# Where the keys' sums of squares are formed in a two-layer attention kernel: four single-column matmuls, or a transposing sum and the fold matmul

## The chip, the cores and the metric

The kernel runs on one core of one Trainium2 chip. The metric is the device time of one execution in microseconds (us), median of several runs. The core has a matrix engine (TensorE, "PE" in the profile, with its weight loads shown apart as "PEld"), and four others that work beside it, each through its own queue in order: VectorE (DVE), ScalarE (ACT), GpSimd (POOL) and SyncE (SP), which issues most of the transfers. Matmul results go to PSUM, everything else lies in SBUF.

## The reference

32 sequences of 64 tokens with 512 features go through two layers; each is a cross attention and a feed-forward part with residual sums. All is in 32-bit floats. What matters here is the second layer's attention, which normalises every query and every key by its root mean square before the scores:

```python
def rmsnorm(x, w, eps=EPS):
    xf = x.astype(jnp.float32)
    var = jnp.mean(xf * xf, axis=-1, keepdims=True)
    return w * (xf * jax.lax.rsqrt(var + eps)).astype(x.dtype)
...
q = rmsnorm(q, q_norm_w)
k = jnp.repeat(k, n_rep, axis=1)
v = jnp.repeat(v, n_rep, axis=1)
k = rmsnorm(k, k_norm_w)
scale = 1.0 / np.sqrt(HEAD_DIM)
scores = jnp.einsum('bhqd,bhkd->bhqk', q, k) * scale + attention_mask
attn = jax.nn.softmax(scores.astype(jnp.float32), axis=-1).astype(q.dtype)
out = jnp.einsum('bhqk,bhkd->bhqd', attn, v)
```

There are 32 query heads and 8 key heads of 128 features. The sum of squares is over these 128 features, so there is one sum for each query of each head and one for each key.

## The kernel before

The 2048 tokens are cut into four chunks of 512 (eight sequences). Each attention layer walks through 32 steps: for each of the 8 key heads `g` the four chunks `c`. A step makes the keys (`project_k`), the four query heads of the group (`project_q`), the values' sum (`values`), the value projection (`project_v`), the first products of the output projection (`output_first`) and the scores of the next step (`scores`); the rest of the output products (`output_rest`) and the softmax, cut into pieces by `yield`, run between them. `run` is software-pipelined: in the turn of step i the keys and queries of step i+1 are projected before the values of step i are formed. A scheduler places the instructions in each engine's queue by the order of the code and waits are by semaphores; each queue is then worked in order.

The names that matter:

- **kT, ksq.** `project_k` (L333) leaves the keys transposed in PSUM: 128 features on the partitions, 512 keys along the row. In the second layer ACT squares them into `ksq` (L355) and DVE scales them into `kT` (L356).
- **quarters, part.** The query projection (L188, tiles `P`) is a seven-product scheme whose result comes in four quarters, called in the order in which the matmuls end. For each, DVE adds two pieces into `qT` (L416), ACT squares that (L418), and DVE makes `part` (L422): a reduction with `apply_transpose=True`, which transposes each 32x32 block and sums along the row, so that 128x512 squares give 128x16 sums over 32 features each. Four such calls fill `part`.
- **pm, fold.** `norms` (L430) puts sums over all 128 features into the PSUM tile `pm`, 20 columns: 16 for the queries, 4 for the keys. For the keys, four matmuls (L440) take a 128x128 block of `ksq` as weights and the column of ones as moving operand. For the queries, four matmuls (L446), j = 0 to 3, take `fold` as weights (128x32, four stacked 32x32 identities), 16 columns of `part` as moving operand, and write 32 rows of `pm` each, so that each uses another group of 32 columns of the array. A 32-bit matmul appears in the trace as two passes, each with a weight load and a matmul: the 4 calls of either kind are 8 loads and 8 matmuls.
- **qs, qr, rb.** DVE copies `pm` with a small constant to `qs` (L456), POOL raises it to the power -1/2 into `qr` (L231), and DVE spreads the queries' part over the columns as `rb` (L280). The keys' part of `qr` and `rb` are multiplied into the scores (L502).

On PE's queue a step of the second layer runs: pk (L340), P (L188), po (`values`, L564), pm (L440, then L446), pv (L366), the first two output products O (L188), S (`scores`, L468), the other five products O. After `qr` POOL forms four sums of blocks of `oT` (`left_sums`, L168 to L171), which output products use; after them it adds the mask to the scores (L512).

Of the kernel before, what the change touches and what calls it, by code (L numbers as in the profile page):

```python
# [9 lines left out]
F32 = mybir.dt.float32  # L10
# [5 lines left out]
ALU = mybir.AluOpType  # L16
AX = mybir.AxisListType

P = 128
# [8 lines left out]
NH = NB // 4  # L28
KB = 32
KH = S // KB  # L30
# [14 lines left out]
def tile_xattn_ffn_2_layers(ctx: ExitStack, tc: tile.TileContext, a: dict, out: bass.AP):  # L45
    nc = tc.nc
# [5 lines left out]
    const = ctx.enter_context(tc.tile_pool(name="const", bufs=1))  # L52
# [3 lines left out]
    sm = ctx.enter_context(tc.tile_pool(name="sm", bufs=2))  # L56
    psp = ctx.enter_context(tc.tile_pool(name="psp", bufs=6, space=bass.MemoryType.PSUM))

    def mm_tile(name):
        return psp.tile([P, CH], F32, tag="mm", name=name)  # L60
# [25 lines left out]
    def tmp_tile(name):  # L86
        return ap_.tile([P, 2, CH], F32, tag="tmp", name=name)
# [15 lines left out]
    def load_ctx(c, name):  # L103
        t = ctx_tile(f"ctxT{name}")
        nc.sync.dma_start(
            t, a["ctxT"][:, c * CH : (c + 1) * CH].rearrange("(k p) t -> p k t", p=P)
        )
        return t
# [37 lines left out]
    fold = const.tile([P, KB], F32, tag="fold", name="fold")  # L146
    nc.gpsimd.memset(fold, 0.0)
    for j in range(4):
        nc.vector.tensor_copy(fold[j * KB : (j + 1) * KB, :], ident[j * KB : (j + 1) * KB, j * KB : (j + 1) * KB])
    ones = const.tile([P, 1], F32, tag="ones", name="ones")  # L150
    nc.gpsimd.memset(ones, 1.0)
    wqk = const.tile([P, 2], F32, tag="wqk", name="wqk")

    def key_weight():
# [10 lines left out]
    def left_sums(t, width=HC, engine=nc.gpsimd):  # L165
        b = [t[:, k, :, 0:width] for k in range(NBLK)]
        tt = engine.tensor_tensor
        tt(b[4], b[2], b[3], ALU.add)  # L168
        tt(b[5], b[4], b[0], ALU.subtract)
        tt(b[2], b[0], b[2], ALU.subtract)  # L170
        return tt(b[6], b[1], b[5], ALU.subtract).ins  # L171

    def right_sums(t):
        b = [t[:, k] for k in range(NBLK)]
        tt = nc.gpsimd.tensor_tensor
        tt(b[4], b[1], b[0], ALU.subtract)
        tt(b[5], b[3], b[4], ALU.subtract)
        tt(b[1], b[3], b[1], ALU.subtract)
        tt(b[6], b[2], b[5], ALU.subtract)
# [49 lines left out]
    def rsqrt(dst, src):  # L229

        nc.gpsimd.tensor_tensor(dst, src, nhalf[:, : src.shape[-1]], ALU.pow)  # L231

    norms = {}
# [43 lines left out]
    def spread(name, cols):  # L277

        out = m2_tile(name)
        nc.vector.transpose(  # L280
            out.rearrange("p (g q) -> p g q", q=KB), cols.unsqueeze(2).to_broadcast([P, 16, KB])
        )
        return out
# [5 lines left out]
    class Attention:  # L289
# [42 lines left out]

        def project_k(self, g, c, ctxT):  # L333

            n = f"{self.L}_{g}_{c}"
            wkv = self.wkv[g]
            kT = ap_.tile([P, CH], F32, tag="kT", name=f"kT{n}", bufs=1)
            ps = mm_tile(f"pk{n}")
            for k in range(KT):
                nc.tensor.matmul(  # L340
                    ps, wkv[:, k, 0, :], ctxT[:, k, :], start=(k == 0), stop=(k == KT - 1)
                )
            if self.L == 0:
                self.rotate(
                    f"rk{n}",
                    ps,
                    lambda t: kT if t is None else t,
                    lambda t: t.rearrange("p (f w) -> p f w", f=NH),
                    lambda tab: tab.rearrange("p e j k -> p (e j k)")
                    .unsqueeze(1)  # L350
                    .to_broadcast([P, NH, 4 * S]),
                )
                return kT, None
            ksq = tmp_tile(f"ksq{n}")[:, 0, :]
            nc.scalar.activation(ksq, ps, AF.Square)  # L355
            nc.vector.tensor_scalar(kT, ps, wqk[:, 0:1], None, ALU.mult)  # L356
            return kT, ksq

        def project_v(self, g, c, ctxT):
            n = f"{self.L}_{g}_{c}"  # L360
# [66 lines left out]
            quarters(n, self.wq[g], xnT[c], quarter)  # L427
            return qT, part

        def norms(self, g, c, ksq, part):  # L430


            if self.L == 0:
                return None
            n = f"1_{g}_{c}"
            NQ, NK = NH * GQ * KH, NH * KH

            pm = mm_tile(f"pm{n}")
            for t in range(NK):
                nc.tensor.matmul(  # L440
                    pm[:, NQ + t : NQ + t + 1], ksq[:, t * P : (t + 1) * P], ones,
                    start=True, stop=True,
                )
            p6 = part.rearrange("p i f (j x) -> p j i f x", j=4)
            for j in range(4):
                nc.tensor.matmul(  # L446
                    pm[j * KB : (j + 1) * KB, 0:NQ].rearrange("p (f i x) -> p i f x", f=NH, i=2),
                    fold,
                    p6[:, j],
                    start=True,  # L450
                    stop=True,
                )
            qs = sm.tile([P, NQ + NK], F32, tag="qs", name=f"qs{n}")
            qr = sm.tile([P, NQ + NK], F32, tag="qr", name=f"qr{n}")

            nc.vector.tensor_scalar(qs, pm[:, 0 : NQ + NK], HD * EPS, None, ALU.add)  # L456
            rsqrt(qr, qs)
            return spread(f"rb{n}", qr[:, 0:NQ]), qr[:, NQ:]
# [174 lines left out]
        def run(self, hooks, joined, after, between=lambda c: None, tail=lambda: None, late={}):  # L633

            steps = [(g, c) for g in range(NKV) for c in range(NCH)]

            def ctx_of(i):  # L640
                return load_ctx(steps[i][1], f"{self.L}_{steps[i][0]}_{steps[i][1]}")

            before = None
            v = self.v
            ctxT = ctx_of(1)
            (kT, ksq), (qT, part) = self.state
            scales = self.norms(0, 0, ksq, part)
            st = self.scores(0, 0, kT, qT)
            for i, (g, c) in enumerate(steps):
                more = i + 1 < len(steps)  # L650
                if c == NCH - 1 and g + 1 < NKV:
                    self.load_kv(g + 1)
                for hook in hooks.get((g, c), ()):
                    hook()
                ctx_next = ctx_of(i + 2) if i + 2 < len(steps) else None
                if g == NKV - 1 and c > 1:
                    between(c - 2)
                pieces = self.softmax(g, c, st, scales)

                def middle():  # L660
                    if c == NCH - 1 and g + 1 < NKV:
                        with tc.issue_after(self.pooled):
                            left_sums(self.wq[g + 1])

                if before is not None:
                    probs = self.output_rest(*before, pieces, middle)
                    with tc.issue_after(self.added):
                        for hook in late.get((g, c), ()):
                            hook()
                else:  # L670
                    *_, probs = pieces
                if c == 0 and g > 0:
                    self.load_out(g)
                done = before is not None and before[0] == NKV - 1
                if done:
                    joined(before[1])
                if more:
                    kT, ksq = self.project_k(*steps[i + 1], ctxT)
                    if c == 0:
                        right_sums(self.wo[g])  # L680
                    qT, part = self.project_q(*steps[i + 1])
                    if c == NCH - 2 and g + 1 < NKV:
                        self.load_q(g + 1)
                else:
                    tail()
                if done:
                    after(before[1])
                oT = self.values(g, c, v, probs)
                if more:
                    scales = self.norms(*steps[i + 1], ksq, part)  # L690
                self.pooled = left_sums(oT)
                if more:
                    v = self.project_v(*steps[i + 1], ctxT)
                before = self.output_first(g, c, oT)
                if more:
                    st = self.scores(*steps[i + 1], kT, qT)
                ctxT = ctx_next
            between(NCH - 2)
            self.output_rest(*before)
            joined(before[1])  # L700
# [601 lines left out]
```

## Time and profile before

| | us |
|---|---|
| median of 3 runs | 2956.05 |
| lowest, highest | 2955.57, 2958.86 |
| the profiled execution, its own time | 2953.24 |
| span of its trace, first to last instruction | 2951.5 |

Busy time in the span of 2951.5 us: PE 2862.5 us (97%), PE's weight loads 2244.8 (76%), DVE 1793.7 (61%), POOL 1282.8 (43%), ACT 820.9 (28%). The second layer's attention is the part from about 1650 us to 2860 us of the span.

How such lines are read: a line of groups gives the source line, the engine, the operation, the tiles written and read, the shapes, the count, then the busy time in us and the mean duration in ns, then the engine's idle time just before these instructions and what ended it. A line of the timeline gives start and length in us of a run of like instructions. The length of a run is from the start of the first to the end of the last, and weight loads and matmuls of a run overlap each other, so counts times durations exceed it. "issue" means that nothing in the trace explains the wait.

### The profile page before, as it was taken

What the parts mean: (1) busy time and instruction counts of PE and PEld (TensorE: products, weight loads), DVE (VectorE), ACT (ScalarE), POOL (GpSimd) and SP (SyncE); (2) the same over time, 40 slices, a digit from 0 to 9 for tenths busy, and PEclk for the clock granted to TensorE, in tenths of its full rate; (3) what the DMA queues carried; (4) which work ended last, traced back from release to release, by engine and by line L of the source; (5) the groups of instructions that cost most, each with busy time, mean ns of one, the idle gap of its engine ahead of it and who ended that gap; (6) DMA issues with size and microseconds to landing.
All of it is one profiled execution on the core that took longest, in us unless ns stands there. A gap on an engine that the chain in (4) does not pass through costs nothing.

```text
span 2951.5 us, 40382 instructions
## 1 busy us (share of the span) xinstructions
PE 2862.5 (97%) x16502; PEld 2244.8 (76%) x16502; DVE 1793.7 (61%) x2720; ACT 820.9 (28%) x1397; POOL 1282.8 (43%) x933
## 2 busy tenths in 40 slices
PE   7999999999999999899999999999999999999987
PEld 5878777788877887667666687888888888888765
DVE  7667777777777767533343655555555555555565
ACT  3323333333333333211111322222222222222232
POOL 5544545454545555422122445353535353535432
PEclk9999999999999999899999999999999999999998
DMA  4111111111111111000000102020202010101001
GB/s 160 40 42 44 52 48 54 49 52 51 44 52 44 51 43 58 22 22 22 22 9 15 36 29 71 29 65 29 65 30 65 29 65 29 65 31 64 15 1 58
DMA packets 103807, 130.71 MB, mean 44 GB/s; under 512 B 8725, under 2 KB 65165, under 8 KB 103623
## 3 DMA queue, kind: packets, MB, share of 16 engines
q1 hardware_dynamic: 103047, 127.09, 13.3%
q8 instruction: 130, 2.13, 0.3%
q10 hardware_dynamic: 576, 1.05, 0.1%
q14 instruction: 54, 0.44, 0.0%
HBM read 123.92 MB, written 4.19 MB: 43 GB/s over the span
## 4 chain that ended last, share of the span: by engine, by line
PE 87%; DVE 8%; issue 2%; ACT 2%; POOL 1%; DMA 0%; ACTq 0%; DVEq 0%; POOLq 0%
PE P L188 32%; PE O L188 23%; PE pv L366 8%; PE pk L340 6%; PE pd L894 5%; PE po L564 4%; PE S L468 4%; DVE x L590 1%; PE pm L440 1%; DVE S L491 1%; PE pqy L1012 1%; ACT rq L381 1%; DVE r2x L523 1%; PE pu L1012 0%; ACT h L211 0%
## 5 line engine op out<-in xcount | busy, mean ns | idle before, releaser
L188 PE MATMUL P<-xnT,wq 128*128 128x256 f32 x3584 | 797.9, 382 | 23.0 <-ACT h L211 21.4
L188 PE MATMUL O<-wo,oT 128*128 128x256 f32 x3584 | 803.6, 382 | 4.2 <-ACT oT L572 3.3
L188 PEld LDWEIGHTS P<-xnT,wq 128*128 128x128 f32 x3584 | 678.1, 191 | 158.5 <-issue 39.3
L188 PEld LDWEIGHTS O<-wo,oT 128*128 128x128 f32 x3584 | 671.5, 190 | 117.4 <-issue 22.1
L590 DVE TENSOR_TENSOR x<-x,O 128x512 f32<-128x512 f32 (+1 forms) x448 | 368.4, 823 | 146.3 <-PE O L188 146.0
L544 POOL TENSOR_TENSOR s<-s,ib 128x512 f32<-128x512 f32 x128 | 169.3, 1343 | 488.0 <-DVE ib L280 479.5
L211 ACT COPY h<-P 128x512 f32<-128x512 f32 (+1 forms) x352 | 200.4, 573 | 365.7 <-PE P L188 362.8
L385 POOL TENSOR_TENSOR qT<-h,rq 128x512 f32<-128x512 f32 x128 | 175.2, 1368 | 276.1 <-DVE rq L384 265.2
L188 PE MATMUL P<-xnT,wgu 128*128 128x256 f32 (+1 forms) x1232 | 273.8, 382 | 0.0
L231 POOL TENSOR_TENSOR qr<-qs,nhalf 128x20 f32<-128x20 f32 x32 | 113.3, 3542 | 347.8 <-DVE qs L456 347.3
L538 ACT ACTIVATE s<-s 128x1024 f32<-128x1024 f32 x64 | 67.7, 1057 | 707.0 <-DVE s L536 707.0
L188 PEld LDWEIGHTS P<-xnT,wgu 128*128 128x128 f32 (+1 forms) x1232 | 228.0, 187 | 47.0 <-issue 7.4
L366 PE MATMUL pv<-wkv,ctxT 128*128 128x128 f32 x1984 | 238.0, 278 | 2.9 <-DVE h L398 1.7
L366 PEld LDWEIGHTS pv<-wkv,ctxT 128*128 128x128 f32 x1984 | 226.2, 192 | 14.3 <-issue 8.9
L381 ACT COPY rq<-h 64x512 f32<-64x512 f32 x256 | 157.9, 617 | 243.8 <-DVE h L398 241.5
L340 PE MATMUL pk<-ctxT,wkv 128*128 128x512 f32 x496 | 223.1, 592 | 0.0
L416 DVE TENSOR_TENSOR qT<-h,P 128x512 f32<-128x512 f32 x128 | 83.9, 674 | 190.0 <-PE P L188 190.0
L883 POOL TENSOR_TENSOR hT<-h,h 128x512 f32<-128x512 f32 (+1 forms) x48 | 55.6, 1178 | 283.5 <-DVE h L876 263.8
L340 PEld LDWEIGHTS pk<-ctxT,wkv 128*128 128x128 f32 x496 | 94.1, 190 | 92.9 <-issue 89.6
L894 PE MATMUL pd<-wd,hT 128*128 128x512 f32 (+1 forms) x352 | 155.0, 592 | 0.0
L383 DVE TENSOR_TENSOR h<-h,cosT 128x512 f32<-128x512 f32 x128 | 90.0, 703 | 104.9 <-ACT rq L381 104.9
L876 DVE TENSOR_TENSOR h<-h,P 128x512 f32<-128x512 f32 (+1 forms) x96 | 59.6, 640 | 152.0 <-PE P L188 103.7
(235 smaller groups left out, 3260.0 us busy)
## 6 DMA issues: line engine op xcount, KB each, us to landing
ctxT<-in_ctxT SPq DMA_DIRECT2D x62, 1024.0 KB
wq<-in_L_wq SPq DMA_DIRECT2D x32, 256.0 KB
wo<-in_L_wo SPq DMA_DIRECT2D x32, 256.0 KB
wq<-in_L_wqT SPq DMA_DIRECT2D x32, 256.0 KB
wo<-in_L_woT SPq DMA_DIRECT2D x32, 256.0 KB
wgu<-in_qweight_gu SPq DMA_DIRECT2D x40, 128.0 KB
out<-o SPq DMA_DIRECT2D x16, 256.0 KB
x<-in_x SPq DMA_DIRECT2D x12, 256.0 KB
```

The lines of the kernel that those rows point to most:

```text
L188: nc.tensor.matmul(pv[0:w, m, :], left[:, l, k, m * P : m * P + w], right[:, r, k, :], start=(first and m == 0 and k == 0), stop=(k == 1), ...
L211: nc.scalar.copy(t[size], ps[size])
L231: nc.gpsimd.tensor_tensor(dst, src, nhalf[:, : src.shape[-1]], ALU.pow)
L340: nc.tensor.matmul(ps, wkv[:, k, 0, :], ctxT[:, k, :], start=(k == 0), stop=(k == KT - 1))
L366: nc.tensor.matmul(ps[:, t * HD : (t + 1) * HD], ctxT[:, k, t * P : (t + 1) * P], wkv[:, k, 1, :], start=(k == 0), stop=(k == KT - 1),)
L381: nc.scalar.copy(t[lo:hi, 1], src[HD - hi : HD - lo])
L385: nc.gpsimd.tensor_tensor(dst(None), dst(x), dst(t[:, 1]), ALU.add)
L468: nc.tensor.matmul(s5[j * KB : (j + 1) * KB, f, e], kT[:, f, e, j], qT[:, f * 4 + j].rearrange("p h q -> p (h q)"), start=True, stop=True,)
L544: nc.gpsimd.tensor_tensor(sv[:, f], sv[:, f], ib[:, f * W : (f + 1) * W].unsqueeze(1).to_broadcast([P, KH, W]), ALU.mult,)
L564: nc.tensor.matmul(po[j][:, f * W : (f + 1) * W], v[rows, f, e], probs[rows, f, e], start=(e == 0), stop=(e == KH - 1),)
L590: self.added = nc.vector.tensor_tensor(dst, dst, src, ALU.add).ins
L894: nc.tensor.matmul(p, hT[0:w_, t, tk * P : (tk + 1) * P], wd[i][0:w_, t, :], start=(t == 0), stop=(t == len(tiles) - 1),)
```

## The change

The keys' sums take the way that the queries' sums take. `project_k` reduces `ksq` by DVE's transposing sum to `kpart` (128x16: for each of 16 blocks of 32 keys one sum over each 32 features), and `norms` brings the four partial sums together with the same `fold` weights, in four matmuls of four columns, each issued right after the query matmul of the same j. The column of ones and the four single-column matmuls go.

```diff
-    ones = const.tile([P, 1], F32, tag="ones", name="ones")
-    nc.gpsimd.memset(ones, 1.0)
...
             nc.scalar.activation(ksq, ps, AF.Square)
             nc.vector.tensor_scalar(kT, ps, wqk[:, 0:1], None, ALU.mult)
-            return kT, ksq
+            part = sm.tile([P, NH * KH * 4], F32, tag="kpart", name=f"kpart{n}")
+            nc.vector.tensor_reduce(
+                part, ksq.rearrange("p (g k) -> p g k", k=KB), AX.X, ALU.add, apply_transpose=True
+            )
+            return kT, part
...
-        def norms(self, g, c, ksq, part):
+        def norms(self, g, c, kpart, part):
...
             pm = mm_tile(f"pm{n}")
-            for t in range(NK):
-                nc.tensor.matmul(
-                    pm[:, NQ + t : NQ + t + 1], ksq[:, t * P : (t + 1) * P], ones,
-                    start=True, stop=True,
-                )
+            k6 = kpart.rearrange("p (x j) -> p j x", j=4)
             p6 = part.rearrange("p i f (j x) -> p j i f x", j=4)
             for j in range(4):
                 nc.tensor.matmul(
                     pm[j * KB : (j + 1) * KB, 0:NQ].rearrange("p (f i x) -> p i f x", f=NH, i=2),
                     fold,
                     p6[:, j],
                     start=True,
                     stop=True,
+                )
+                nc.tensor.matmul(
+                    pm[j * KB : (j + 1) * KB, NQ : NQ + NK], fold, k6[:, j], start=True, stop=True
                 )
```

The callers pass `kpart` on in place of `ksq`. In the first layer `norms` returns at once, and nothing changes.

More of the change, by code (lines that the diff above doesn't have):

```diff
@@ L645, in run @@
             ctxT = ctx_of(1)
-            (kT, ksq), (qT, part) = self.state
-            scales = self.norms(0, 0, ksq, part)
+            (kT, kpart), (qT, part) = self.state
+            scales = self.norms(0, 0, kpart, part)
             st = self.scores(0, 0, kT, qT)
@@ L677, in run @@
                 if more:
-                    kT, ksq = self.project_k(*steps[i + 1], ctxT)
+                    kT, kpart = self.project_k(*steps[i + 1], ctxT)
                     if c == 0:
@@ L689, in run @@
                 if more:
-                    scales = self.norms(*steps[i + 1], ksq, part)
+                    scales = self.norms(*steps[i + 1], kpart, part)
                 self.pooled = left_sums(oT)
```

## The prediction

> **What bounds the kernel now.** I read the page's shares first, then the chain of waits over two steps of the second attention, then its timeline, then the groups of the four lines that the change touches.
>
> ```profile
> PE 2862.5 (97%) x16502; PEld 2244.8 (76%) x16502; DVE 1793.7 (61%) x2720; ACT 820.9 (28%) x1397; POOL 1282.8 (43%) x933
> ...
> 2019.72 12.17 PE P L188 x56
> 2031.88 1.94 PE po L564 x32
> 2033.82 0.98 PE pm L440 x8
> 2034.81 0.18 PE pm L446 x8
> 2034.99 3.77 PE pv L366 x32
> ...
> 2070.45 0.98 PE pm L440 x8
> 2071.43 0.19 PE pm L446 x8
> 2071.62 3.77 PE pv L366 x32
> ```
>
> The chain runs through PE alone, and the same place returns after 2070.45 - 2033.82 = 36.63 us. So what PE's queue loses in a step is gained, if nothing else comes to end last. The removed matmuls hold the chain for 0.98 us, the remaining fold for 0.18.
>
> What lies beside them is seen in the timeline:
>
> ```profile
> 2020.39 0.75 DVE L356 TENSOR_SCALAR kT<-pk,wqk 128x512 f32<-128x512 f32 x1 [0.27 <-ACT ksq L355]
> 2023.28 0.69 DVE L416 TENSOR_TENSOR qT<-h,P 128x512 f32<-128x512 f32 x1 [2.14 <-PE P L188]
> ...
> 2031.42 1.25 DVE L416 TENSOR_TENSOR qT<-h,P 128x512 f32<-128x512 f32 x2
> 2031.81 1.61 PEld L564 LDWEIGHTS po<-s,v 32*128 32x128 f32 x32 [0.33 <-issue]
> 2032.11 1.29 ACT L418 ACTIVATE q<-qT 128x512 f32<-128x512 f32 x2 [0.88 <-DVE qT L416]
> 2032.77 1.37 DVE L422 TRANSPOSE_TENSOR_REDUCE part<-q 128x16 f32<-128x512 f32 x2
> 2033.75 0.97 PEld L440 LDWEIGHTS pm<-ones,ksq 128*128 128x128 f32 x8 [0.33 <-DVE part L422]
> 2034.73 0.16 PEld L446 LDWEIGHTS pm<-part,fold 128*32 128x32 f32 x8
> 2034.92 1.19 PEld L366 LDWEIGHTS pv<-wkv,ctxT 128*128 128x128 f32 x10
> 2035.06 0.18 DVE L456 TENSOR_SCALAR qs<-pm 128x20 f32<-128x20 f32 x1 [0.92 <-PE pm L446]
> 2035.32 3.54 POOL L231 TENSOR_TENSOR qr<-qs,nhalf 128x20 f32<-128x20 f32 x1 [12.57 <-DVE qs L456]
> ```
>
> The last `part` ends at 2032.77 + 1.37 = 2034.14. That is 0.39 us after PE started L440, and 0.59 before the fold, which reads it. So the single-column matmuls do hidden service: they fill the time in which DVE finishes the last quarter. The 0.33 ahead of L440 is put down to `part`, yet the last `part` was still running; the same 0.33 stands before po with "issue". It is the change of the array's shape, not a wait for DVE. In 28 of the 32 steps these distances are the same to 0.03 us, the weight load of pv following L440's first by 1.17.
>
> **The change, part by part.**
>
> ```profile
> L440 PEld LDWEIGHTS pm<-ones,ksq 128*128 128x128 f32 x256 | 31.1, 191 | 10.8 <-DVE part L422 9.6 <-issue 1.1
> L446 PEld LDWEIGHTS pm<-part,fold 128*32 128x32 f32 x256 | 5.0, 108 | 0.5
> L422 DVE TRANSPOSE_TENSOR_REDUCE part<-q 128x16 f32<-128x512 f32 x128 | 89.3, 710 | 46.3 <-ACT q L418 43.3
> L356 DVE TENSOR_SCALAR kT<-pk,wqk 128x512 f32<-128x512 f32 x32 | 23.6, 739 | 8.7 <-ACT ksq L355 8.7
> ```
>
> *Removed on PE:* 8 passes a step, 2034.73 - 2033.75 = 0.98 us, 31.4 in 32 steps. Taking all of it as gain would be the mistake to make.
>
> *Added on DVE:* one `kpart` a step, the same form as L422: 0.71 us, 22.7 in all. In the new order it stands right behind `kT` in 30 steps, and the first `qT` add is behind it, for whose Square ACT waits. `kT` ends at 2021.14 and that add starts at 2023.28, since it waits for PE's product: 2.14 us free, and 1.5 in the tightest of the ordinary steps. So it costs nothing; without that cover it would be 0.71 a step for the first quarter, which is not the one the fold waits for. DVE is busy for 569 of 1050 us in this stage (54%), then for 56%. Of the two other steps, one has it between two parts of the softmax's maximum, one between norm statistics; up to 0.7 each could show, and I leave both out of the sum. ACT's square and `kT` stay. No DMA is touched, and neither SP's queue nor POOL's is passed; POOL loses one 0.10 us memset at the start, long before it waits 8.75 us for DVE.
>
> *The new wait.* The fold is now first after po, and its first matmul waits for the last `part`. Behind it in PE's queue stand pv, O and S. It can load at 2034.14 plus the signal's way; elsewhere in this trace a weight load that waits for DVE alone starts 0.05 after DVE's end, so at 2034.19. Without that wait it would be 2033.75, so PE idles 0.44 us more per step. From 2034.19 to the present start of pv, 2034.92, are 0.73 us: the new fold must be shorter than this to gain at all.
>
> *The fold with 16 passes instead of 8.* Now it takes 2034.92 - 2034.73 = 0.185. The eight loads of 0.108 are over in 0.16, so the last starts 0.05 after the first: the four column groups start 0.007 apart, and the second pass of a group follows its first by 0.029. Another 0.136 passes from the last load to pv's. The change doubles the passes of each group, but alternates query and key matmul on the same group. The trace has no such alternation, so bounds. Below, every group runs its own four passes beside the others: last load at 0.02 + 3 x 0.029 = 0.107, plus 0.136 = **0.24 us**. In the middle, the key matmul holds up the next group until its own group is free: five turns of two passes, 9 x 0.029 + 0.136 = 0.40. Above, at the distance of L440's full-width passes (0.97 - 0.19 = 0.78 for seven, 0.11 each): 15 x 0.11 + 0.136 = 1.8. I take the lower one: the trace shows the first pass of the fourth group loading before the second pass of the first group, so groups already run side by side, and the rows of this very operation are nearer than L440's.
>
> The Trainium skill says otherwise ("TensorE: Matmul & The Clock Gate", Part 3, "The mechanism"): matmuls start and end in program order, without reordering. By that rule the alternating passes would queue up one behind another, which is a rival below. The order of the present passes does not look so, if each call's two passes are adjacent in the program, which the trace does not tell.
>
> *Sum.* 0.73 - 0.24 = 0.49 us a step, 28 x 0.486 = 13.6 us. The first two and the last two steps have other waits; the first two differ by some tenths either way, and in the last ones DVE's own queue sets `qs`, so I count nothing. The profiled execution took 2953.24 (span 2951.5 and 1.7 around it): 2939.6 for one like it. It is 2.8 below the median of the runs shown; against that, 2956.05 - 13.6 = **2942.4**.
>
> *Does it stay gained?* pv follows the fold as now, and `qs` again 0.14 after pv's first load, so POOL's chain (3.54 for `qr`, then four sums) moves with PE. oT's copies on ACT end at 2035.95, before the first O at 2038.49. The next step's P waits on ACT only for copies of PE's own products. All of these shift together.
>
> **The rivals.**
> 1. *Groups held up in turn:* fold 0.40, gain 0.33 a step, 9.2 in all: 2946.8. For it: one queue of instructions feeds all groups. Against it: nothing shown.
> 2. *Strict order of passes:* 16 loads, those of one group 0.029 apart and the next group following at once: 4 x (3 x 0.029 + 0.002) = 0.356, plus 0.136 = 0.49. Gain 0.24 x 28 = 6.7: 2949.4. Against it: the eight present loads, starting within 0.05.
> 3. *Each change of operand on a group drains it* (the slower side): every one of the 8 matmuls then pays its two passes, 0.055, and the 0.11 that separate the last fold matmul from pv: 1.32 us. That is 0.59 over the 0.73, 16.5 us in all: 2972.6. It decides once the fold exceeds 0.73 us. For it: the 0.33 that PE pays at changes of shape. Against it: shape and weights stay the same here.
> 4. *No new wait:* `part` is somehow ready and the fold starts at 2033.75: 1.17 - 0.24 = 0.93 a step, 26 us: 2930. Against it: the DVE chain after the last P product, 2034.14, which the change does not shorten.
> 5. *DVE's added work reaches the path* through a later first quarter: the gain falls by what exceeds 1.5 to 2.1 us of cover; no change, about 2954.
>
> **How the numbers follow.** Lower bound of the fold 48%, rival 1 22%, rival 2 13%, rival 3 8%, rival 4 3%, rival 5 6%. Predicted is the first, 2942.4; its own range is 2939 to 2945. For 8 in 10 I go from 2938 to 2951, past rivals 1 and 2. What a measurement here can tell from no change is about 0.2%, 5.9 us, so faster means under 2950.1: the first, rivals 1 and 4 and most of 2, 0.81; the same: the rest of 2, and 5, 0.11; slower: rival 3, 0.08.
>
> **What the profile after would show.** L440 gone; 512 loads of 32 columns in its place; before the first of a step PE's loads idle about 0.77 us (0.33 and 0.44), ended by `part`; pv's first load 0.24 after the fold's first and 0.30 after the last `part`; steps at 36.14 us; 32 `kpart` of 0.71, with the first `qT` add still waiting for P. It would be wrong if the fold takes over 0.73 us, if `part` itself ends later against po, or if a later wait in the step grows by what was gained.

## The result and the profile after

The changed kernel takes 2942.05 us (median of 5 runs, 2938.55 to 2943.32) against 2956.05 of the kernel before beside it (5 runs, 2953.59 to 2958.86). The ratio is 0.9948, with an interval of 0.9937 to 0.9959: about half a per cent faster. The profiled execution took 2943.32, with a span of 2941.5.

The chain of waits over the same place, one step of the second attention (start, length, what; line numbers have moved by up to 3):

```profile
2018.75 9.59 PE P L186 x44
...
2030.53 0.58 DVE qT L419
2031.12 0.02 issue
2031.14 0.64 ACT q L421
2031.78 0.02 issue
2031.80 1.38 DVE part L425 x2
2033.18 0.04 issue
2033.23 0.27 PE pm L445 x7
2033.50 0.06 PE pm L452 x5
2033.56 3.77 PE pv L369 x32
...
2054.91 5.18 PE P L186 x24
```

Where the chain before ran through PE alone, it now leaves PE for 4.9 us before the fold: the row of adds, squares and reductions of the last quarters ends at 2033.18, later than po (its last matmul ends at 2032.86). From one start of P to the next are 2054.91 - 2018.75 = 36.16 us; before, the same place came again after 36.62.

The timeline of the same step, with DVE's new instruction:

```profile
2019.42 0.75 DVE L355 TENSOR_SCALAR kT<-pk,wqk 128x512 f32<-128x512 f32 x1 [0.27 <-ACT ksq L354]
2020.09 0.70 DVE L357 TRANSPOSE_TENSOR_REDUCE kpart<-ksq 128x16 f32<-128x512 f32 x1
...
2022.32 0.69 DVE L419 TENSOR_TENSOR qT<-h,P 128x512 f32<-128x512 f32 x1 [1.52 <-PE P L186]
...
2031.80 1.37 DVE L425 TRANSPOSE_TENSOR_REDUCE part<-q 128x16 f32<-128x512 f32 x2
2033.23 0.15 PEld L445 LDWEIGHTS pm<-part,fold 128*32 128x32 f32 x6 [0.77 <-DVE part L425]
2033.23 0.27 PE L445 MATMUL pm<-part,fold 128*32 128x16 f32 x7 [0.37 <-DVE part L425]
...
2033.31 0.17 PE L452 MATMUL pm<-kpart,fold 128*32 128x4 f32 x1
...
2033.49 3.65 PEld L369 LDWEIGHTS pv<-wkv,ctxT 128*128 128x128 f32 x32
```

The added reduction eats into idle time: DVE still stands 1.52 us before the first add into `qT`, waiting for PE's product as before (then 2.14). PE's loads idle 0.77 before the fold, 0.33 for the change of the array's shape and 0.44 for `part`. From the first load of the fold to pv's are 0.26 us. The sum closes: before, pv's first load came 1.167 us after the first of `pm`; now it comes 0.438 + 0.262 = 0.700 after the same place, which is 0.467 less, as much as the step lost.

In groups (as before: idle time ahead, and what ended it):

```profile
L357 DVE TRANSPOSE_TENSOR_REDUCE kpart<-ksq 128x16 f32<-128x512 f32 x32 | 22.3, 698 | 0.0
L452 PEld LDWEIGHTS pm<-kpart,fold 128*32 128x32 f32 x256 | 6.0, 113 | 0.0
L445 PEld LDWEIGHTS pm<-part,fold 128*32 128x32 f32 x256 | 5.8, 108 | 23.9 <-DVE part L425 21.6 <-issue 1.4 <-PE po L566 0.9
```

The 31 us of single-column weight loads are gone, 6 us of small ones came, and the idle time ahead of `pm` rose from 10.8 to 23.9 us. This wait takes 13 us of the 25 that the table of busy times would promise.

The two profiled spans differ by 9.9 us, the medians by 14.0. By the first weight load of each `pm`: up to the first one +3.25, over the first two steps -0.05, over the 27 distances from the third `pm` to the thirtieth 992.46 to 979.88, which is -12.58, and in the rest -0.55. Of the 3.25, 2.73 are there before the second layer begins (its first `ksq` starts at 1650.82 and at 1653.55), in code that the change does not touch; the other 0.52 lie just ahead of the first `pm`, where PE's loads now idle 0.76 us instead of 0.24 and the profile names no cause. The windows from 1150 to 1210 us, where the first attention hands over to the feed-forward part, show the 2.73; first the kernel before, then the changed one (busy times by engine, then the granted clock, the DMA share and GB/s):

```profile
1150.00:1210.00 60.00, 46.76 (x283) 35.16 (x284) 43.84 (x61) 15.86 (x28) 36.13 (x27) 0.86 0.17 53
```

```profile
1150.00:1210.00 60.00, 46.17 (x270) 33.96 (x271) 41.67 (x60) 15.90 (x28) 34.18 (x26) 0.80 0.18 53
```

The changed kernel's execution was granted 0.80 of the clock there, the other 0.86; in the 430 us that follow both had 1.00. The ten profiled executions of this document differ in the same way, and not by kernel: from DVE's last `rk<-pk,cosT` in the first layer to the second layer's first `ksq` they take 507.1 to 507.2 us in the four with 0.86, 508.1 to 508.4 in the four with 0.83 or 0.84, and 510.5 and 509.9 in the two with 0.81 and 0.80. One of the four with 0.86 (kfirst) has the change too. This is a reason to read the step from one fold to the next rather than the span. That step is what the experiments compare.

### The profile page after: what moved, and what is told of

Same layout as the page of the kernel before. It is cut to its first block, busy times and chain, and to the rows that moved or that the text cites. A ratio compares the mean times of both kernels' runs of the same rounds, so it can differ in the third digit from the quotient of the medians.

```text
span 2941.5 us, 40415 instructions
## 1 busy us (share of the span) xinstructions
PE 2838.8 (97%) x16502; PEld 2217.1 (75%) x16502; DVE 1812.1 (62%) x2752; ACT 820.2 (28%) x1397; POOL 1283.9 (44%) x932
## 4 chain that ended last, share of the span: by engine, by line
PE 80%; DVE 12%; ACT 3%; issue 2%; POOL 2%; DMA 0%; DVEq 0%; ACTq 0%; POOLq 0%
PE P L186 30%; PE O L186 22%; PE pv L369 8%; PE pk L339 6%; PE pd L896 5%; PE S L470 4%; DVE part L425 2%; PE po L566 2%; DVE x L592 2%; DVE qT L419 1%; ACT q L421 1%; ACT rq L384 1%; DVE S L493 1%; PE pqy L1014 1%; DVE r2x L525 1%
```

## The experiments

The theory is that of the prediction: PE's queue sets the end, the fold must wait for the last `part`, and the matmuls on the four column groups run side by side. The main rival is that the gain is simply the matrix time removed. "Step" is the distance from the first matmul of one `pm` to the next, the median of the 27 distances from the third `pm` to the thirtieth: 36.625 us before, 36.158 after.

| run | median us | ratio to the kernel before, interval | step us | expected step |
|---|---|---|---|---|
| changed kernel | 2942.05 | 0.9948, 0.9937 to 0.9959 | 36.158 | 36.14 |
| kfirst | 2938.76 | 0.9936, 0.9921 to 0.9951 | 36.085 | 36.08 |
| grouped | 2939.80 | 0.9938, 0.9923 to 0.9953 | 36.137 | 36.13 to 36.16 |
| onescol_last | 2966.23 | 1.0029, 1.0020 to 1.0039 | 36.977 | 36.97 |
| kpart_only | 2956.35 | 0.9993, 0.9983 to 1.0002 | 36.625 | 36.63 |
| kpart_four | 2942.79 | 0.9955, 0.9942 to 0.9969 | 36.158 | 36.16 |
| norms_mid | 2968.83 | 1.0047, 1.0031 to 1.0062 | 36.876 | 37.0 |
| pv_split | 2935.34 | 0.9929, 0.9917 to 0.9942 | 35.910 | 35.82 |
| pv_split_kfirst | 2934.67 | 0.9927, 0.9914 to 0.9939 | 35.900 | as pv_split |

**Did the single-column matmuls fill a wait?** The kernel before, with nothing but the order of `pm`'s eight matmuls turned round:

```diff
-            for t in range(NK):
-                nc.tensor.matmul(
-                    pm[:, NQ + t : NQ + t + 1], ksq[:, t * P : (t + 1) * P], ones,
-                    start=True, stop=True,
-                )
             p6 = part.rearrange("p i f (j x) -> p j i f x", j=4)
             for j in range(4):
...
+            for t in range(NK):
+                nc.tensor.matmul(
+                    pm[:, NQ + t : NQ + t + 1], ksq[:, t * P : (t + 1) * P], ones,
+                    start=True, stop=True,
+                )
```

> The kernel before, with the query folds put ahead of the four single-column matmuls; no instruction added or removed. Theory (the single-column matmuls filled the wait for the last part): PE stands idle until the last part, 0.44 us more, then runs the fold (0.19, a change of shape included) and eight full-width passes (0.89): pv 0.35 us later than before, steps of 36.97 instead of 36.63, about 10 us slower, 2966. Rival (what counts is PE's busy time): same as before, 2956.

Its timeline:

```profile
2037.80 1.37 DVE L422 TRANSPOSE_TENSOR_REDUCE part<-q 128x16 f32<-128x512 f32 x2
...
2039.22 0.16 PEld L441 LDWEIGHTS pm<-part,fold 128*32 128x32 f32 x8 [0.77 <-DVE part L422]
...
2039.40 0.97 PEld L449 LDWEIGHTS pm<-ones,ksq 128*128 128x128 f32 x8
...
2040.29 1.87 PEld L366 LDWEIGHTS pv<-wkv,ctxT 128*128 128x128 f32 x16
```

The same instructions, and every step is 0.35 us longer: the fold starts 0.05 after `part` here too, with 0.77 idle ahead, and the full-width passes come behind it instead of into the gap. Matrix time alone cannot explain that; the rival falls.

**Does DVE's added reduction cost anything?** First alone, in the kernel before (its result is read by nobody):

```diff
             nc.vector.tensor_scalar(kT, ps, wqk[:, 0:1], None, ALU.mult)
+            unused = sm.tile([P, NH * KH * 4], F32, tag="kpart", name=f"kpart{n}")
+            nc.vector.tensor_reduce(
+                unused, ksq.rearrange("p (g k) -> p g k", k=KB), AX.X, ALU.add, apply_transpose=True
+            )
```

> The kernel before, with DVE's 32 reductions of the key squares added into a tile that nobody reads; the single-column matmuls stay. Theory (DVE has 1.5 to 2.1 us free there): steps stay at 36.63, 2956, DVE 22 us busier. Rival (DVE's added work reaches the path): up to 0.7 a step, 20 us slower.

The step is 36.625 us as without it, and the interval of the ratio holds 1. Then four times in the changed kernel, more than the idle time holds:

```diff
-            nc.vector.tensor_reduce(
-                part, ksq.rearrange("p (g k) -> p g k", k=KB), AX.X, ALU.add, apply_transpose=True
-            )
+            for _ in range(4):
+                nc.vector.tensor_reduce(
+                    part, ksq.rearrange("p (g k) -> p g k", k=KB), AX.X, ALU.add, apply_transpose=True
+                )
```

> The changed kernel with each reduction of the key squares done four times. It adds 3 x 0.70 = 2.1 us of DVE time a step where 1.5 are free, so the first add into qT starts about 0.6 late. Theory (the first quarter is not the one that the fold waits for): steps stay at 36.16 in the ordinary steps; a us or two more around the first and last ones. Rival (DVE's time counts as soon as the cover is gone): 0.6 a step, 17 us slower than the changed kernel, 2959.

Its timeline on DVE:

```profile
2019.58 0.75 DVE L355 TENSOR_SCALAR kT<-pk,wqk 128x512 f32<-128x512 f32 x1 [0.26 <-ACT ksq L354]
2020.25 2.94 DVE L358 TRANSPOSE_TENSOR_REDUCE kpart<-ksq 128x16 f32<-128x512 f32 x4
2023.11 0.65 DVE L420 TENSOR_TENSOR qT<-h,P 128x512 f32<-128x512 f32 x1
2024.46 0.71 DVE L426 TRANSPOSE_TENSOR_REDUCE part<-q 128x16 f32<-128x512 f32 x1 [0.70 <-ACT q L422]
2028.60 0.69 DVE L420 TENSOR_TENSOR qT<-h,P 128x512 f32<-128x512 f32 x1 [3.43 <-PE P L186]
```

The first add now waits for nothing and comes 3.53 us after the start of `kT` instead of 2.90, so 0.63 late. The second again waits 3.43 for PE: the lateness is gone before the last quarter, and the step does not move. Only one of the 27 distances is longer, by 0.35; DVE had stood idle for 3.27 us before the second add there, so it was not DVE's work, and what it was stays open. So the reduction is covered twice, by the idle time ahead of the first quarter and by that between the first and the second.

**How do the 16 passes of the fold run?** Query matmuls first, then key matmuls:

```diff
                     start=True,
                     stop=True,
                 )
+            for j in range(4):
                 nc.tensor.matmul(
                     pm[j * KB : (j + 1) * KB, NQ : NQ + NK], fold, k6[:, j], start=True, stop=True
                 )
```

> The changed kernel with the four query matmuls of the fold first and the four key matmuls behind them. Theory (column groups run side by side, alternation costs nothing): the fold stays at 0.24 to 0.26 us from its first load to pv's, steps of 36.13 to 36.16. Rival (alternating on one group holds up the others): the fold falls below 0.22.

The fold lasts 0.238 us instead of 0.262, and the step is shorter by 0.021. So alternating costs 0.024, not the 0.16 or 0.25 of the two rivals that let one group hold up the others. The other way round, the loop over the four key matmuls comes first and that over the query matmuls second. The key matmuls need not wait for `part`:

> The changed kernel with the four key matmuls of the fold put ahead of the four query matmuls. Theory (PE's queue sets the end, the fold waits for the last part, column groups run side by side): the key matmuls need no part, so they run 0.30 us after po, inside the idle time; only the query matmuls are left behind the last part, 0.19 instead of 0.26. Gain 0.08 a step over the changed kernel: steps of 36.08 us instead of 36.16, some 2 us in all, about 2940. Rival (the gain is the matrix time that was removed): the same matmuls, the same time, steps of 36.16.

The chain of waits in this run:

```profile
2026.88 1.38 DVE part L425 x2
2028.25 0.04 issue
2028.30 0.26 PE pm L449 x8
2028.55 3.77 PE pv L369 x32
```

Only the eight passes of the queries are left behind `part`. The step falls by 0.073; over 28 steps that is 2.0 us, which the intervals of the times can't separate from the changed kernel, but the steps can.

**Can the wait be filled again?** The whole of pv ahead of the fold:

```diff
                 if more:
-                    scales = self.norms(*steps[i + 1], kpart, part)
-                self.pooled = left_sums(oT)
-                if more:
                     v = self.project_v(*steps[i + 1], ctxT)
+                    scales = self.norms(*steps[i + 1], kpart, part)
+                if more and self.L == 1:
+                    with tc.issue_after(self.rooted):
+                        self.pooled = left_sums(oT)
+                else:
+                    self.pooled = left_sums(oT)
                 before = self.output_first(g, c, oT)
```

(`rooted` is POOL's power; its order against POOL's sums stays as it was.)

> The changed kernel with the fold put behind pv on PE, and POOL's four sums of oT kept behind the power. Theory: the wait for part is gone there (pv 0.44 earlier, a change of shape of 0.2 paid instead, about 0.24 gained), but qs and the power come 3.3 us later, POOL adds the mask 2 us later, DVE's maximum and the output addition queued behind it too, and the last output product waits about 1 us for that addition: steps of 37.0, slower than the changed kernel by some 20 us. Rival (the chain over POOL has room): steps of 35.92, about 2935.

Its timeline:

```profile
2043.89 3.54 POOL L229 TENSOR_TENSOR qr<-qs,nhalf 128x20 f32<-128x20 f32 x1 [14.10 <-DVE qs L458]
...
2051.22 1.27 POOL L169 TENSOR_TENSOR oT<-oT 128x512 f32<-128x512 f32 x1
2052.45 2.48 POOL L514 TENSOR_TENSOR s<-s,mask 128x512 f32<-128x512 f32 x2
2054.97 1.25 DVE L525 TRANSPOSE_TENSOR_REDUCE r2x<-s 128x32 f32<-128x1024 f32 x1 [3.26 <-POOL s L514]
2056.14 0.65 DVE L592 TENSOR_TENSOR x<-x,O 128x512 f32<-128x512 f32 x1
...
2056.84 1.59 PEld L186 LDWEIGHTS O<-wo,oT 128*128 128x128 f32 x8 [1.09 <-DVE x L592]
```

The stall moved rather than went: power, sums, mask, maximum and the addition queued behind the maximum each come later, and the last output product waits 1.09 us for that addition. Each step is 0.72 longer than the changed kernel's. Whether another order on POOL would avoid this was not tried.

A quarter of pv, eight of its 32 passes, is enough to fill the gap:

```diff
                 if more:
+                    if first:
+                        pv = self.project_v(*steps[i + 1], ctxT, range(first))
                     scales = self.norms(*steps[i + 1], kpart, part)
...
                 if more:
-                    v = self.project_v(*steps[i + 1], ctxT)
+                    v = self.project_v(*steps[i + 1], ctxT, range(first, TT), pv)
```

(`first` is 1 in the second layer; `project_v` takes the tiles to form and a PSUM tile begun earlier. POOL's sums are tied behind the power as above.)

> The changed kernel with the first of pv's four tiles (eight passes, 0.89 us) put ahead of the fold, and POOL's sums kept behind the power. Theory: this fills PE's wait for the last part. pv starts 0.30 after po, a change of shape of about 0.2 follows, the fold takes 0.26, then 24 passes: the first O product 0.34 earlier, steps of 35.82, about 9.5 us faster than the changed kernel, 2932.5. The power comes 0.55 later, within the 1.4 us that the output additions have to spare. Rival (that room is not there): the 0.34 is given back at the last output product.

Its timeline:

```profile
2028.64 1.37 DVE L428 TRANSPOSE_TENSOR_REDUCE part<-q 128x16 f32<-128x512 f32 x2
2029.62 0.97 PEld L369 LDWEIGHTS pv<-wkv,ctxT 128*128 128x128 f32 x8 [0.33 <-DVE part L428]
...
2030.71 0.16 PEld L448 LDWEIGHTS pm<-part,fold 128*32 128x32 f32 x7
...
2030.97 2.75 PEld L369 LDWEIGHTS pv<-wkv,ctxT 128*128 128x128 f32 x24
```

No wait for DVE is left there: `part` was done 0.70 before the fold began, the 0.33 is again the change of shape, and the chain of waits of this step is PE's alone. The step is 35.910, 0.25 shorter than the changed kernel's instead of the expected 0.34. The terms expected were right: 0.89 for eight passes and 0.2 for a change of shape make 1.09 us, and 1.09 lie between pv's first load and the fold's. But the 0.44 of wait that goes, less the 0.2, is 0.24; the 0.34 was added up wrongly. No output product waits more than before. With the key matmuls first:

> As the run with pv split, with the key matmuls of the fold ahead of the query matmuls. Theory: with the wait filled, nothing is left for the order to gain: the same to 0.03 a step. Rival: another 0.08 a step as without the split.

35.900: 0.010 less, within the 0.03 expected, since the order now only shortens the fold itself, from 0.258 to 0.248 us. At 2934.67 us this is the fastest median measured here, 0.9927 of the kernel before; the 2935.34 of the run ahead of it can't be told from it.

## Why the prediction was right

- *What bounds.* PE's queue, with 36.63 a step: shown by the step's following the changes to PE's order, and not following 0.70 or 2.94 us of DVE's work. Where it did not follow PE alone, in norms_mid, the chain of waits ran over POOL.
- *Removed, 0.98 a step, and the new wait that takes part of it.* Predicted idle ahead of the fold 0.77, found 0.77; fold 0.05 after `part`, found 0.053 in the ordinary steps. That the single-column matmuls filled this time is shown by onescol_last.
- *The fold with 16 passes.* The term that was mis-sized: 0.243 predicted by the lower bound, 0.262 measured. The alternation, which the bound left at nothing, accounts for it: by the grouped run it costs 0.024, and without it the fold takes 0.238. The sum for 28 steps is therefore 28 x 0.467 = 13.1 us instead of 13.6.
- *DVE's 0.71 at nothing.* Right, by kpart_only; its price without cover, which I had put on the first quarter and not on the fold, did not reach the step in kpart_four, with the first add 0.63 us late.
- *Does it stay gained?* Yes: the step fell by what the place of `pm` lost. How near the chain over POOL lies is shown by norms_mid.
- *The rivals.* Groups held up in turn, strict order and a drain at each change of operand fall with the fold's 0.262 us: they stood at 0.40, 0.49 and 1.32. By strict order, with the distances of rival 2, the step would be 36.39 by estimate. The Trainium skill states such an order ("TensorE: Matmul & The Clock Gate", Part 3, "The mechanism"): matmuls start and end in the order of the program. The trace does not agree: the program has a key call right behind each query call, but seven of the eight query passes start before the first key pass (2033.31 in the timeline of the step above), and the step is 36.158. How the two passes of a call stand in PE's queue, no run here shows. That no new wait arises falls with the 0.44 us, and DVE's work on the path with kpart_only.
- *The first and last steps, counted as nothing.* Right by luck in part: at the first `pm`, over the first two steps and in the rest they gave +0.52, -0.05 and -0.55, which cancel.
- *The time.* 2942.4 against 2942.05 is nearer than the working deserves, and that is luck: the medians of the kernel before, beside later runs, were 2958.32 and 2955.15. For the profiled execution 2939.6 was forecast and 2943.32 measured; 2.73 of these 3.7 us lie in the stretch with the lower granted clock.

## What to carry to other kernels

Before counting removed work as gain, look at what the next instruction on the same queue waits for: here 0.98 us of matmuls went, and 0.44 of it came back as a wait for a result that they had been hiding. Such a gap can be filled with a piece of later work that needs nothing new, but a piece larger than the gap delays whatever waits for the result: here a quarter of the value projection ahead of the fold gained 0.25 us a step, all of it lost 0.72. And work added to another engine was free here because that engine waits for the bounding one afterwards; the wait before its next instruction is the first measure, the wait before the instruction that matters is the real one.

## What the runs showed of the hardware

- A 32-bit matmul's two passes on one group of 32 columns do not keep other groups from starting: sixteen passes on four groups took 0.238 us, to the next load, with the groups in turn and 0.262 with two calls on each group in succession.
- At a change of the array's shape, the time from the start of the last matmul to the next weight load grows with that matmul's columns: 0.101 us after the fold's 4 columns (changed kernel), 0.110 after 16 (kernel before), 0.203 after 128 of pv (pv_split) and 0.303 after 256 of po.
- The granted clock in one 60 us stretch, 0.86 in one profiled execution and 0.80 in the other, goes with a difference of 2.73 us at code that is the same in both; over ten executions it lay between 0.80 and 0.86, and the two lowest were the longest there.
